# A graph layer on one core: the first loads are asked for earlier, and two more groups of edges are brought by ScalarE and VectorE

## The chip, the cores and the metric

The kernel runs on one core of a Trainium2 chip. The core has five engines with queues of their own: TensorE (PE, with weight loads as PEld), VectorE (DVE), ScalarE (ACT), GpSimd (POOL) and SyncE (SP), which here only issues DMAs. The metric is the device time of one execution in microseconds, the median of several.

## The reference

One layer of a graph network over 12,500 nodes and 400,000 edges, with edges sorted by their target:

```python
h = jnp.maximum(_layernorm(x, axis=-1), 0.0)          # 12500 x 128
s, d = edge_index                                      # 400000 each, d sorted
m = relu(concat([h[s], h[d], edge_attr_32], -1) @ w1 + b1) @ w2 + b2
agg = segment_sum(m, d, num_segments=12500)
gi = agg @ w_ih + b_ih ; gh = h @ w_hh + b_hh          # gates r, z, n of a GRU
out = x + (1 - z) * n + z * h
```

The product with w1 is split: the part of the source is A = h @ w1[0:128], that of the target with the bias is B = h @ w1[128:256] + b1, and the part of the edge's 32 features stays a product per edge. w2 is applied after the sum, per node.

## The kernel before

**First stage.** Nodes come in 14 batches (`load`, L370). VectorE makes the statistics, ScalarE the normalised rows, TensorE turns them and multiplies them with w1; A is written back to memory (`A<-asb`, L482), and three batches of B (`batch_store`). The turned h of all nodes stays on the chip as `hT_all`. The loop runs over 26 chunks, `q`, of up to four tiles. In it also the edge sources of some groups are loaded, one row of 1024 numbers each (`at_row`, L423).

**Edges.** The 3125 tiles of 128 edges make NP = 391 groups of eight (group 0 has five), and each group two units `u`. For each group three things are loaded by SP: for every two groups a tile `L` (`fetch`, L567), which has the places of the targets in its upper 64 partitions (`dstP`, each row copied to 32 partitions) and the features of the edges in the lower 64; and for every group 2 x 32 rows of B into one of four tiles `RW` (`window_rows`, L600), whose lower half holds the weights of the features. VectorE makes a one-hot of the places in `L` (L586), and one product of `L` and `RW` gives the target's and the features' part for 256 columns (L683, tile `pre`). The source's part comes in one of these ways:

- from GpSimd: eight indirect gathers of 128 rows of A into a tile `G` (L163, 11 buffers); VectorE adds it to the product, with the relu (L713). The first nine groups are gathered from x instead, because A is not there yet, and are normalised and turned;
- by ScalarE ("act", 28 groups): 1024 copies of one column of `hT_all` each into `HE_act` (L979), 16 numbers of columns per register load. TensorE multiplies the tile with w1 into `pre` (L694) and ScalarE does the relu (L725);
- by VectorE ("dve", 27 groups): 512 instructions that join two columns each (L986) and 8 copies that part them again (L991) into `HE_dve`;
- by SP ("sp", 5 groups): 1024 DMAs of one row of A each (L968).

After the relu in `RB`, TensorE sums the edges of a node with another one-hot (`seg`, L739). Every 14 groups a block of nodes is finished (`node`, L790): gates, sigmoid, tanh, output, and one batch of B for later groups.

**Order.** The schedule is written by hand: each engine does its instructions in the order of the program, unit after unit (`stages`, L1040; the loop at L1075). `run_jobs` (L1007) spreads a job by hand evenly over the units of its span, four portions per unit. A job for group k ends at unit 2k − 4, four units before the group's first unit; the next one of the same engine starts there. `SPREAD`, `START` and the loop at L92 choose the groups:

```python
SPREAD = {"dve": 27, "act": 28, "sp": 5}
START = {"dve": 14, "act": 4, "sp": 24}
...
        lo, hi = START[m] // 2 + 2, NP - {"dve": 5, "act": 3, "sp": 12}[m]
        for i in range(n):
            k = lo + int((i + 1) * (hi - lo) / n)
```

With this ScalarE has groups 17, 31, 45, ... 388, VectorE 22, 36, ... 386, and the spans have 26 or 28 units. The pool `pj` holds `HE_act` and `HE_dve`, two buffers each, and lies beside the first stage's tiles; the pool `p3`, which holds the three buffers of `L`, takes the memory that the first stage gives back. The first loads for the edges stand after the first stage (L1032):

```python
    gathers(0)
    dst_tile(1)
    for q in range(3):
        fetch(q)
    for k in range(4):
        window_rows(k)
```

Of the kernel before, what the change touches and what calls it, by code (L numbers as in the profile page):

```python
# [11 lines left out]
I32 = mybir.dt.int32  # L12
# [40 lines left out]
PIECE = 128  # L53
STEP = {"act": 4, "dve": 8, "sp": 4}
ROW = 4 * D
SPREAD = {"dve": 27, "act": 28, "sp": 5}
START = {"dve": 14, "act": 4, "sp": 24}
NR = 12672

H_AT = 16512  # L60

# [2 lines left out]
def tile_gnn(ctx: ExitStack, tc: tile.TileContext, x, src, srcT, dstT, dstP, eaT, eaP, w1, b1, w2T, b2,  # L64
# [23 lines left out]
        return [(t0 + a * GRP + j, j, a) for j in (2 * h, 2 * h + 1) for a in range(2)  # L88
                if t0 + a * GRP + j < t1]

    mode, order = {}, {m: [] for m in SPREAD}
    for m, n in SPREAD.items():  # L92
        lo, hi = START[m] // 2 + 2, NP - {"dve": 5, "act": 3, "sp": 12}[m]
        for i in range(n):
            k = lo + int((i + 1) * (hi - lo) / n)
            while k in mode:
                k += 1
            mode[k] = m
            order[m].append(k)


    src_i = {}
# [86 lines left out]
    nc.vector.memset(brow, 0.0)  # L189
    b1b = const.tile([128, D], F32, name="b1b")  # L190
    base_d = at[96:97, :NP - 1]
    by_hand = [k for m in ("sp", "act", "dve") for k in order[m]]
    NJ = len(by_hand)
    place_of = const.tile([NJ, 2], F32, name="place_of")
    for i, (to_sp, to_others) in enumerate(((ROW, 4), (0, H_AT))):
# [107 lines left out]
    def setup(pool):  # L303
# [45 lines left out]
        yield  # L349
        place(0)  # L350

    st_all = const.tile([128, NT, 2], F32, name="st_all")
    nc.vector.memset(st_all[:, NFULL, :], 0.0)
    with tc.tile_pool(name="pp", bufs=3) as pp:
# [85 lines left out]
        for q in range(NC + 3):  # L440
            if q < NC:
                b, i0, c, e, P, n0 = chunk(q)
                if c == 0:
                    stat(b + 2)
                    fin(b + 1)
            if 1 <= q <= NC:
                b, i0, c, e, P, n0 = chunk(q - 1)
                pts[q - 1] = SEGB[q % 2]
                for j in range(c, e):
                    nc.tensor.transpose(pts[q - 1][:, (j - c) * P:(j - c + 1) * P],  # L450
                                        xs[b][:P, j, :], ident[:P, :P])
                if e == bats[b][1]:
                    load(b + 5)
            if q >= 3:
                b, i0, c, e, P, n0 = chunk(q - 3)
                if c == 0:
                    asb[b] = pp.tile([128, 8, D], F32, name="asb", bufs=2)
                nc.scalar.copy(asb[b][:P, c:e, :], pas.pop(q - 3)[:P, :e - c, :])
            if q < NC:
                b, i0, c, e, P, n0 = chunk(q)  # L460
                for j in range(c, e):
                    relu_norm(xs[b][:P, j, :], xs[b][:P, j, :], st_all[:P, i0 + j, :])
                if e == bats[b][1]:
                    sqr(b + 2)
            if 1 <= q <= NC:
                b, i0, c, e, P, n0 = chunk(q - 1)
                copy = nc.scalar.copy if q % 4 == 0 else nc.vector.tensor_copy
                copy(columns(b, c, e), pts.pop(q - 1)[:, :(e - c) * P].rearrange(
                    "f (i p) -> f i p", i=e - c))
            if q >= 4:  # L470
                for _ in range(3):
                    at_row()
            if q >= 6:
                next(setting, None)
            if q in (6, 8, 10):
                batch_product(q // 2 - 3, pp, "bt", 1)
            if q in (7, 9, 11):
                batch_store(q // 2 - 3)
            if q >= 3:
                b, i0, c, e, P, n0 = chunk(q - 3)  # L480
                if e == bats[b][1]:
                    nc.sync.dma_start(nodes(A, i0, e, P), asb[b][:P, :e, :])  # L482
            if 2 <= q <= NC + 1:
                b, i0, c, e, P, n0 = chunk(q - 2)
                pas[q - 2] = ps2.tile([128, PAIR, D], F32, name="pre")
                for j in range(c, e):
                    nc.tensor.matmul(pas[q - 2][:P, j - c, :], columns(b, j, j + 1)[:, 0, :],
                                     w1a, start=True, stop=True)
# [72 lines left out]
        nc.vector.tensor_copy(flag, f[:, 6:7])  # L561


    Ls, OH, RT, HE, SEG = ({} for _ in range(5))
    hand = {}

    def fetch(q):  # L567
        if q * QP >= NP:
            return
        n = min(QP, NP - q * QP)  # L570
        c = slice(q * QP * 512, (q * QP + n) * 512)
        Ls[q] = p3.tile([128, QP * 512], F32, name="L")
        p = dstP[:, c]
        nc.sync.dma_start(
            Ls[q].bitcast(I32)[:2 * V, :n * 512],
            bass.AP(tensor=p.tensor, offset=p.offset, ap=[list(p.ap[0]), [0, V], [1, n * 512]]))
        nc.sync.dma_start(Ls[q][2 * V:, :n * 512], eaP[:, c])

    def onehot_T(k):
        if k >= NP:  # L580
# [8 lines left out]
                                    accum_out=dlast[:2 * V, n:n + 1])  # L589


    bases = {}

    def block(k):
        return max(b for b in range(NB) if BLOCKS[b][0] <= k)

    def slot(b, i):
        return i // 2 if b < NB - 1 else (BP - BLOCKS[b][1]) // 2 + i // 2

    def window_rows(k):  # L600
        if k >= NP:
            return
        b = block(k)
        k0, n, _ = BLOCKS[b]
        if k == k0:
            _, vals = nc.values_load_multi_w_load_instructions(
                base_i[0:1, b, 0:n], engines=[ET.SP], min_val=0, max_val=4 * D * LAST,
                skip_runtime_bounds_check_because="clamped above")
            for i, v in enumerate(vals):
                bases[k + i] = v  # L610
        v = bases.pop(k)
        for a in range(2):
            nc.sync.dma_start(RW[k % 4].bitcast(U8)[V * a:V * (a + 1), a, :],
                              B_bytes[bass.ds(v + 4 * D * SHIFT * a, 4 * D * V)].rearrange(
                                  "(p f) -> p f", p=V))

    def onehot(k):
        if k >= NP or (k % 2 and k > 1):
# [330 lines left out]
    def one_by_one(m, k):  # L949
        et = {"act": ET.Activation, "dve": ET.DVE, "sp": ET.SP}[m]  # L950
        r = by_hand.index(k)
        if m == "sp":
            goal[k] = tc.alloc_semaphore(f"brought{r}"), 16 * PAIR * 128
            G[k] = pj.tile([128, GRP, 2, D], F32, name="G_sp", bufs=1)
            rows = G[k].bitcast(U8)
        else:
            hand[k] = pj.tile([128, PAIR * 128], F32, name=f"HE_{m}")
            he = hand[k].bitcast(U8)
        for e0 in range(0, PAIR * 128, LOAD[m]):
            low, high = (0, ROW * (N - 1)) if m == "sp" else (H_AT, H_AT + 4 * (N - 1))  # L960
            _, vals = nc.values_load_multi_w_load_instructions(
                at[r:r + 1, e0:e0 + LOAD[m]], engines=[et], min_val=low, max_val=high,
                skip_runtime_bounds_check_because="src holds numbers of nodes")
            if m == "sp":
                for i, v in enumerate(vals):
                    e = e0 + i
                    a, j = divmod(e // 128, GRP)
                    fetched = nc.sync.dma_start(rows[e % 128:e % 128 + 1, j, a, :],  # L968
                                                A_bytes[bass.ds(v, ROW)].rearrange("(o f) -> o f", o=1))
                    fetched.then_inc(goal[k][0], 16)  # L970
                    tc.no_tile_sem_insts.add(fetched.ins.name)
                    tc.add_to_no_dep_group(f"rows{k}", fetched.ins)
                    if i % STEP[m] == STEP[m] - 1:
                        yield
                continue
            if m == "act":
                for i, v in enumerate(vals):
                    e = e0 + i
                    nc.scalar.copy(he[:, e * 4:e * 4 + 4], column(v))  # L979
                    if i % STEP[m] == STEP[m] - 1:  # L980
                        yield
                continue
            if e0 % PIECE == 0:
                both = pj.tile([128, PIECE // 2, 4], U16, name="both")
            for i in range(0, LOAD[m], 2):
                nc.vector.scalar_tensor_tensor(both[:, (e0 % PIECE + i) // 2, :], column(vals[i + 1]),  # L986
                                               256.0, column(vals[i]), op0=ALU.mult, op1=ALU.add)
                if i % STEP[m] == STEP[m] - 2:
                    if (e0 + i + 2) % PIECE == 0:
                        p0 = e0 + LOAD[m] - PIECE  # L990
                        nc.vector.tensor_copy(  # L991
                            he[:, p0 * 4:(p0 + PIECE) * 4].rearrange("p (n c b) -> p n c b", c=2, b=4),
                            both.bitcast(U8).rearrange("p n (b c) -> p n c b", c=2))
                    yield
# [12 lines left out]
    def run_jobs(u, phase):  # L1007
        if phase == 0:
            for m, k, span in jobs.get(u, ()):
                live[m] = [one_by_one(m, k), u, span, PAIR * 128 // STEP[m], 0]  # L1010
        for m, job in list(live.items()):
            it, start, span, steps, done = job
            want = -(-steps * ((u - start) * PH + phase + 1) // (span * PH))
# [17 lines left out]

    gathers(0)  # L1032
    dst_tile(1)
    for q in range(3):
        fetch(q)
    for k in range(4):
        window_rows(k)


    def stages(u):  # L1040
# [248 lines left out]
```

## Time and profile before

| | us |
|---|---|
| median of 3 runs | 3385.01 (3376.61 to 3388.27) |
| the profiled execution | 3383.87 |
| its span | 3382.1 |

| engine | busy us | share of the span |
|---|---|---|
| PE | 2400.4 | 71% |
| DVE | 2213.6 | 65% |
| ACT | 3081.1 | 91% |
| POOL | 2542.8 | 75% |

In the rows of the profile the columns are: line, engine, operation, tile written and tiles read, count, then busy time in us and the mean of one in ns, then the idle time of the engine just before these instructions and what ended it. "issue" is idle time in which the engine waited for nothing that the profile shows, such as register loads of its own sequencer; these are not counted as busy. In a timeline a row has its start and its length in us, and in brackets the idle time before it. In a row of a table of stretches stand the stretch, its length, the busy time and count of PE, PEld, DVE, ACT and POOL, the clock granted to TensorE as a part of full speed, the busy share of the 16 DMA engines and GB/s. A row of waits has who waited, on what, the total in us, how often, and the longest.

### The profile page before, as it was taken

The numbers are of one execution on the slowest core, as the hardware profiler recorded it, in microseconds if no ns is written. First come the engines' busy times: TensorE is split into PE (matmuls) and PEld (weight loads), VectorE is DVE, ScalarE is ACT, GpSimd is POOL, SyncE is SP. The second block draws the span as 40 slices with busy tenths as digits, with TensorE's granted clock in tenths as the row PEclk, the third lists the DMA queues.
The fourth block names the chain that finished last, engine by engine and source line by source line (L and its number), as shares of the span: only waits on it lengthen the run. The fifth ranks groups of instructions, "written<-read, shape, count | busy, mean of one in ns | idle before, by whom it ended". The sixth has DMA issues, their size and how long they took to land. (4 is left out here: it accounts for less than half of the span.)

```text
span 3382.1 us, 93395 instructions
## 1 busy us (share of the span) xinstructions
PE 2400.4 (71%) x13113; PEld 1554.8 (46%) x13113; DVE 2213.6 (65%) x16274; ACT 3081.1 (91%) x29057; POOL 2542.8 (75%) x2654
## 2 busy tenths in 40 slices
PE   7567766776677677668776777677667767766767
PEld 6444444444444444445444444444444444444445
DVE  8566666766666666666667766666656666666665
ACT  7599899999999998998999999999889998988975
POOL 7777777777777777777777777777777777777775
PEclk9778777887888777877877878787777787778778
DMA  6433444444444444444444444444444444343332
GB/s 215 104 92 84 95 99 101 99 97 103 96 95 99 97 98 95 99 104 97 96 98 97 98 95 105 97 99 98 95 98 96 100 95 99 94 96 94 92 94 67
DMA packets 196737, 335.77 MB, mean 99 GB/s; under 512 B 69445, under 2 KB 118148, under 8 KB 196112
## 3 DMA queue, kind: packets, MB, share of 16 engines
q0 software_dynamic: 84640, 173.51, 23.0%
q1 hardware_dynamic: 111327, 156.18, 17.8%
q14 instruction: 517, 4.23, 0.4%
q8 instruction: 109, 1.79, 0.2%
q10 hardware_dynamic: 144, 0.07, 0.0%
HBM read 309.25 MB, written 20.24 MB: 97 GB/s over the span
## 5 line engine op out<-in xcount | busy, mean ns | idle before, releaser
L163 POOL DMA_INDIRECT G<-A,src_i x2576 | 2475.8, 961 | 790.4 <-issue 761.2
L979 ACT COPY HE_act<-hT_all 128x4 uint8 x28672 | 2889.0, 189 | 52.9 <-issue 29.1
L986 DVE SCALAR_TENSOR_TENSOR both<-hT_all 128x4 uint16 x13824 | 1174.3, 154 | 930.3 <-issue 925.6
L683 PE MATMUL pre<-RW,L 128*128 128x256 f32 x3128 | 1136.1, 489 | 461.3 <-DMA RW<-B 237.7
L683 PEld LDWEIGHTS pre<-RW,L 128*128 128x128 f32 x3128 | 662.8, 237 | 736.8 <-issue 420.2
L739 PE MATMUL seg<-RB,OH 128*32 128x129 f32 x6250 | 592.7, 319 | 244.2 <-DVE RB L713 211.9
L739 PEld LDWEIGHTS seg<-RB,OH 128*32 128x32 f32 x6250 | 328.0, 123 | 590.7 <-DVE RB L713 310.1
L713 DVE CUSTOM_DVE_ANT_0 RB<-pre,G 128x1024 f32<-128x1024 f32 x323 | 391.1, 1211 | 70.9 <-DMA G<-A,src_i 56.5
L586 DVE TENSOR_SCALAR L<-L,node_of 64x512 f32<-64x512 int32 x382 | 185.9, 487 | 62.2 <-DMA L<-in_dstP 59.9
L725 ACT ACTIVATE RB<-pre 128x1024 f32<-128x1024 f32 x64 | 65.0, 1016 | 91.0 <-PE pre L694 91.0
L633 DVE TENSOR_TENSOR OH<-dloc,seg 128x512 f32<-128x512 f16 (+1 forms) x198 | 132.3, 669 | 0.0
L765 PE MATMUL nd<-spot,sums 128*128 128x40 f32 x782 | 119.6, 326 | 3.6 <-DVE sums L748 3.6
L765 PEld LDWEIGHTS nd<-spot,sums 128*128 128x128 f32 x782 | 115.5, 237 | 12.7 <-issue 8.8
L991 DVE COPY HE_dve<-both 128x512 uint8<-128x512 uint8 x216 | 97.6, 452 | 7.4
L244 PE MATMUL nd<-w1b,hT_all 128*128 128x128 f32 x224 | 49.4, 368 | 73.1 <-DVE xb L850 73.1
L734 PE MATMUL seg<-zrow 1*128 1x129 bf16 x196 | 45.5, 232 | 78.1 <-DVE OH L633 78.0
L694 PEld LDWEIGHTS pre<-w1a,HE_dve 128*128 128x128 f32 x432 | 89.1, 255 | 12.4
L694 PEld LDWEIGHTS pre<-w1a,HE_act 128*128 128x128 f32 x448 | 85.9, 238 | 11.0
L694 PE MATMUL pre<-w1a,HE_dve 128*128 128x128 f32 x432 | 85.4, 333 | 0.0
L694 PE MATMUL pre<-w1a,HE_act 128*128 128x128 f32 x448 | 83.7, 319 | 0.0
L163 POOL DMA_INDIRECT G<-in_x,src_i x69 | 65.6, 950 | 21.9 <-issue 20.7
L244 PEld LDWEIGHTS nd<-w1b,hT_all 128*128 128x128 f32 x224 | 35.2, 231 | 85.5 <-DVE xb L850 80.0
(177 smaller groups left out, 1346.2 us busy)
## 6 DMA issues: line engine op xcount, KB each, us to landing
G_sp<-A SPq DMA_DIRECT2D x5120, 0.5 KB
L<-in_dstP SPq DMA_DIRECT2D x195, 256.0 KB
L<-in_eaP SPq DMA_DIRECT2D x195, 256.0 KB
G<-A,src_i POOLq DMA_INDIRECT x2576, 2.5
RW<-B SPq DMA_DIRECT2D x782, 16.0 KB
xb<-in_x SPq DMA_DIRECT2D x26, 256.0 KB
out<-xb SPq DMA_DIRECT2D x26, 256.0 KB
xs<-in_x SPq DMA_DIRECT2D x11, 512.0 KB
```

Of the source, the lines that this page charges most:

```text
L163: fetched = nc.gpsimd.indirect_dma_start(out=G[k][:, j, a, :], out_offset=None, in_=table, in_offset=bass.IndirectOffsetOnAxis(ap=src_i[c] ...
L244: nc.tensor.matmul(pm[:m, i:i + D], hT_all[:, n0 + i:n0 + i + m], w1b, start=True, stop=True)
L586: nc.vector.tensor_scalar(o, i, node_of[:, k:k + 1], None, op0=ALU.is_equal)
L633: nc.vector.tensor_tensor(p, dloc[:, e0:e1, None].to_broadcast(shape), row[:, None, :].to_broadcast(shape), op=ALU.is_equal)
L683: nc.tensor.matmul(p[:, 2 * i:2 * i + 2, :], Ls[k // QP][:, c0:c0 + 128], RW[k % 4], start=True, stop=not raw)
L694: nc.tensor.matmul(p[:, 2 * i + a, :], cols, w1a, start=False, stop=n + 1 == len(l) or l[n + 1][1] != j)
L713: made = nc.vector._custom_dve(TENSOR_ADD_SAT, out=o, in0=p, in1=G[k].rearrange("p j a f -> p (j a) f")[:, c, :], s0=float("inf"), s1=0.0)
L739: nc.tensor.matmul(p[r0:r0 + V, :D + 1], OH[k][:, a * GRP + j, :], RB[k % 2][:, 2 * j + a, :D + 1], start=False, stop=all(b != a for _, _, ...
L765: nc.tensor.matmul(p[:, bass.ds(offs[i], V + SHIFT)], sums[:, slot(b, i), :D], spot[:, i % 2, :], start=False, stop=i == len(offs) - 1)
L979: nc.scalar.copy(he[:, e * 4:e * 4 + 4], column(v))
L986: nc.vector.scalar_tensor_tensor(both[:, (e0 % PIECE + i) // 2, :], column(vals[i + 1]), 256.0, column(vals[i]), op0=ALU.mult, op1=ALU.add)
L991: nc.vector.tensor_copy(he[:, p0 * 4:(p0 + PIECE) * 4].rearrange("p (n c b) -> p n c b", c=2, b=4), both.bitcast(U8).rearrange("p n (b c) ...
```

## The change

It has two parts.

The first loads for the edges move into the first stage. `fetch` and `window_rows` are defined before it, at q = 16 the rows of B of groups 0 to 3 are asked for, and at q = 18, 20 and 22 the tiles `L` of groups 0 to 5. Since the pool of `L` is not open then, the first two of these tiles are the two buffers of `HE_dve` and the third is one of `HE_act`. The block at L1034 to L1037 goes.

ScalarE has 29 groups instead of 28, VectorE 27 as before, and group 389 (NP − 2) is brought by both: ScalarE copies columns 0 to 511 and VectorE brings 512 to 1023 into one tile of the name `HE_dve`. The groups are spread anew, over 29.5 and 27.5 shares up to group 389: ScalarE's spans are 26 units but for one of 24 and three of 28, and 12 for its half; VectorE's are 26 and 28, and 14 for its half. GpSimd gathers 329 groups instead of 331.

```diff
-SPREAD = {"dve": 27, "act": 28, "sp": 5}
+SPREAD = {"dve": 27, "act": 29, "sp": 5}
+SHARED, CUT = NP - 2, 512
...
-    mode, order = {}, {m: [] for m in SPREAD}
+    def share(m, k):
+        return (0, PAIR * 128) if k != SHARED else (0, CUT) if m == "act" else (CUT, PAIR * 128)
+
+    mode, order = {SHARED: "both"}, {m: [] for m in SPREAD}
     for m, n in SPREAD.items():
-        lo, hi = START[m] // 2 + 2, NP - {"dve": 5, "act": 3, "sp": 12}[m]
+        lo, hi = START[m] // 2 + 2, NP - 12
+        part = 0
+        if m != "sp":
+            hi, part = SHARED, (share(m, SHARED)[1] - share(m, SHARED)[0]) / (PAIR * 128)
         for i in range(n):
-            k = lo + int((i + 1) * (hi - lo) / n)
+            k = lo + int((i + 1) * (hi - lo) / (n + part))
...
+        order[m] += [SHARED] if part else []
...
+        if q < 3:
+            Ls[q] = pj.tile([128, QP * 512], F32, name="HE_dve" if q < 2 else "HE_act")
+        else:
+            Ls[q] = p3.tile([128, QP * 512], F32, name="L")
...
+            if q == 16:
+                for k in range(4):
+                    window_rows(k)
+            if q in (18, 20, 22):
+                fetch((18, 20, 22).index(q))
...
-            hand[k] = pj.tile([128, PAIR * 128], F32, name=f"HE_{m}")
+            if k not in hand:
+                hand[k] = pj.tile([128, PAIR * 128], F32, name="HE_dve" if k == SHARED else f"HE_{m}")
             he = hand[k].bitcast(U8)
-        for e0 in range(0, PAIR * 128, LOAD[m]):
+        for e0 in range(*share(m, k), LOAD[m]):
...
     gathers(0)
     dst_tile(1)
-    for q in range(3):
-        fetch(q)
-    for k in range(4):
-        window_rows(k)
```

More of the change, by code (lines that the diff above doesn't have):

```diff
@@ L191, in tile_gnn @@
     base_d = at[96:97, :NP - 1]
-    by_hand = [k for m in ("sp", "act", "dve") for k in order[m]]
+    by_hand = order["sp"] + order["act"] + [k for k in order["dve"] if k != SHARED]
     NJ = len(by_hand)
@@ L350, in setup, with fetch, block, window_rows @@
         place(0)
+    Ls = {}
+    def fetch(q):
+        if q * QP >= NP:
+            return
+        n = min(QP, NP - q * QP)
+        c = slice(q * QP * 512, (q * QP + n) * 512)
+        if q < 3:
+            Ls[q] = pj.tile([128, QP * 512], F32, name="HE_dve" if q < 2 else "HE_act")
+        else:
+            Ls[q] = p3.tile([128, QP * 512], F32, name="L")
+        p = dstP[:, c]
+        nc.sync.dma_start(
+            Ls[q].bitcast(I32)[:2 * V, :n * 512],
+            bass.AP(tensor=p.tensor, offset=p.offset, ap=[list(p.ap[0]), [0, V], [1, n * 512]]))
+        nc.sync.dma_start(Ls[q][2 * V:, :n * 512], eaP[:, c])
+    bases = {}
+    def block(k):
+        return max(b for b in range(NB) if BLOCKS[b][0] <= k)
+    def window_rows(k):
+        if k >= NP:
+            return
+        b = block(k)
+        k0, n, _ = BLOCKS[b]
+        if k == k0:
+            _, vals = nc.values_load_multi_w_load_instructions(
+                base_i[0:1, b, 0:n], engines=[ET.SP], min_val=0, max_val=4 * D * LAST,
+                skip_runtime_bounds_check_because="clamped above")
+            for i, v in enumerate(vals):
+                bases[k + i] = v
+        v = bases.pop(k)
+        for a in range(2):
+            nc.sync.dma_start(RW[k % 4].bitcast(U8)[V * a:V * (a + 1), a, :],
+                              B_bytes[bass.ds(v + 4 * D * SHIFT * a, 4 * D * V)].rearrange(
+                                  "(p f) -> p f", p=V))
     st_all = const.tile([128, NT, 2], F32, name="st_all")
@@ L561, in check_windows @@
         nc.vector.tensor_copy(flag, f[:, 6:7])
-    Ls, OH, RT, HE, SEG = ({} for _ in range(5))
+    OH, RT, HE, SEG = ({} for _ in range(4))
     hand = {}
[L567 to L577, printed above, removed]
     def onehot_T(k):
@@ L589, in onehot_T @@
                                     accum_out=dlast[:2 * V, n:n + 1])
-    bases = {}
-    def block(k):
-        return max(b for b in range(NB) if BLOCKS[b][0] <= k)
     def slot(b, i):
         return i // 2 if b < NB - 1 else (BP - BLOCKS[b][1]) // 2 + i // 2
[L600 to L615, printed above, removed]
     def onehot(k):
@@ L1009, in run_jobs @@
             for m, k, span in jobs.get(u, ()):
-                live[m] = [one_by_one(m, k), u, span, PAIR * 128 // STEP[m], 0]
+                e0, e1 = share(m, k)
+                live[m] = [one_by_one(m, k), u, span, (e1 - e0) // STEP[m], 0]
         for m, job in list(live.items()):
```

## The prediction

> **What bounds the kernel now.** I read the page for the sums, then the start's timeline, the busy time by stretch, and the waits of ScalarE and VectorE early and late.
>
> ```profile
> span 3382.1 us, 93395 instructions
> L163 POOL DMA_INDIRECT G<-A,src_i x2576 | 2475.8, 961 | 790.4 <-issue 761.2
> L979 ACT COPY HE_act<-hT_all 128x4 uint8 x28672 | 2889.0, 189 | 52.9 <-issue 29.1
> L986 DVE SCALAR_TENSOR_TENSOR both<-hT_all 128x4 uint16 x13824 | 1174.3, 154 | 930.3 <-issue 925.6
> L713 DVE CUSTOM_DVE_ANT_0 RB<-pre,G 128x1024 f32<-128x1024 f32 x323 | 391.1, 1211 | 70.9 <-DMA G<-A,src_i 56.5
> L725 ACT ACTIVATE RB<-pre 128x1024 f32<-128x1024 f32 x64 | 65.0, 1016 | 91.0 <-PE pre L694 91.0
> L991 DVE COPY HE_dve<-both 128x512 uint8<-128x512 uint8 x216 | 97.6, 452 | 7.4
> ```
>
> GpSimd's gathers: 2475.8 busy plus 790.4 before them is 3266.2 us for 2576, 1.268 each, and nearly all of the 790.4 is "issue", its own rhythm. Its first and last gather of A, from the view of that line:
>
> ```profile
> L163 POOL DMA_INDIRECT G<-A,src_i x2576: 940/944/1601, 92.8 to 3355.0; - x199
> ```
>
> So GpSimd works without a break from 92.8 to 3356, and the rest of the kernel ends 26 us later. But it is not the bound everywhere. Waits of VectorE and ScalarE, first for 142.6 to 2272 us, then for 2272 to 3347.6:
>
> ```profile
> DVE L L586 <- DMA L<-in_dstP: 50.2, 21, 5.9
> ACT gt L824 <- PE nd L818: 44.9, 10, 9.0
> ACT RB L725 <- PE pre L694: 26.2, 15, 5.0
> ACT gt L836 <- PE misc L818: 2.0, 1, 2.0
> ACT gt L834 <- DVE gt L831: 0.2, 1, 0.2
> ```
> ```profile
> DVE RB L713 <- DMA G<-A,src_i: 56.3, 26, 4.4
> ACT RB L725 <- PE pre L694: 60.7, 10, 12.4
> ACT gt L824 <- PE nd L818: 18.3, 9, 3.7
> ACT gt L834 <- DVE both L986: 4.2, 1, 4.2
> ```
>
> VectorE waits for gathered rows only after 2272 us. Until then GpSimd is ahead and the other engines set the pace among themselves; they catch up, and from 2272 on GpSimd sets it. The first add of a gathered group is late because the pipeline starts late:
>
> ```profile
> L713 DVE CUSTOM_DVE_ANT_0 RB<-pre,G x323: 680/1215/1226, 203.6 to 3361.7; 128x1024 f32<-128x1024 f32 x161, 128x512 f32<-128x512 f32 x1
> ```
>
> The start, in order of time:
>
> ```profile
> 90.21 0.66 SPq L574 DMA_DIRECT2D L<-in_dstP  x1
> 92.84 0.94 POOL L163 DMA_INDIRECT G<-A,src_i  x1 [3.18 <-DMA L<-in_dstP]
> 100.32 0.48 DVE L586 TENSOR_SCALAR L<-L,node_of 64x512 f32<-64x512 int32 x1 [9.76 <-DMA L<-in_dstP]
> 118.39 1.19 PE L683 MATMUL pre<-RW,L 128*128 128x256 f32 x2 [11.73 <-DMA RW<-B]
> 124.86 0.94 POOL L163 DMA_INDIRECT G<-A,src_i  x1 [2.34 <-PE misc L666]
> ```
>
> After the first stage VectorE stands 9.76 us for the first L, then TensorE 11.73 us for B's rows, and this even costs GpSimd 2.34 us for a buffer. By stretch (busy time of each engine, clock, DMA share, GB/s):
>
> ```profile
> 0.00:88.70 88.70, 67.56 (x320) 62.19 (x320) 71.92 (x376) 61.77 (x144) 66.03 (x77) 0.96 0.67 212
> 142.60:3347.60 3205.00, 2284.26 (x12480) 1457.43 (x12479) 2102.74 (x15709) 2995.44 (x28857) 2433.19 (x2532) 0.79 0.41 97
> 3347.60:3382.10 34.50, 24.36 (x171) 15.84 (x169) 9.29 (x20) 2.73 (x6) 6.49 (x7) 0.91 0.10 27
> ```
>
> 142.6 and 3347.6 are the first and last column copy of ScalarE. Its waits between them are the two lists above: 73.3 + 83.2 = 156.5 us. So ScalarE works 3205.0 − 156.5 = 3048.5 us there.
>
> **The change, part by part.**
>
> *Early loads.* L of groups 0 to 5 and the four RW tiles are issued in the first stage, into buffers that nobody holds then. The two stalls, 9.76 + 11.73 = 21.5 us, go; what is next late is VectorE's own statistics work, which the 21.5 leave in place. SP's queue gets 6 L issues, 8 RW issues and one register load ahead of the last stores of A, and two more rows of edge sources of 4 KB. At 0.66 us for an L issue (row above) and less than that for the rest, below 14 × 0.66 = 9 us spread over some 25 us, in which SP also waits for ScalarE's copies; GpSimd's first gather of A stands behind those stores (its 3.18 us wait). The bytes: 1.7 MB, which at the 212 GB/s of the first row is 8.0 us of the DMA engines. Their share there is 0.67, so a third of the time is free and most of this fits. Bounds: 0 and 8.0 later; I take 2, nearer to 0 because of that free third. Without the cover the full 8 falls on everything.
>
> [...] With no free share, the start would give 21.5 − 8 and not 21.5 − 2. The trace shows 0.67, not 1, and so stands with the smaller cost.
>
> *GpSimd.* 60 groups by other means become 62 (29 + 27 + 5 + the shared one), 16 gathers fewer: 16 × 1.268 = 20.3 us. With the 2.34 us, its work ends 22.6 us earlier: 3382.1 − 22.6 = 3359.5 plus the 2 above, if nothing else is slower. What is next late is ScalarE.
>
> *ScalarE.* 1.5 more groups. One costs 2889.0/28 = 103.2 us of copies and 52.9/28 = 1.9 us before them: 105.1. So 157.6, plus two more relus (57 groups by hand after 55) at 1.016: 159.6. Its work becomes 3048.5 + 159.6 = 3208 us, as long as the stretch with all its waits was. It starts 21.5 earlier, at 121.1, and without any wait ends its last copy at 3329. Then the tail: the last job now is for group 389, not 388. From TensorE's first products for 389 to the end it was
>
> ```profile
> 3352.72 1.03 PE L683 MATMUL pre<-RW,L 128*128 128x256 f32 x4
> ```
>
> 3382.1 − 3352.7 = 29.4 us, with TensorE at work most of it (24.36 of the last 34.5); eight products with copied columns are added, under 1 us. That gives 3329 + 30 = 3359 without waits.
>
> How many waits stay? ScalarE's jobs ran from unit 4 to 772, 384 groups: 7.94 us of work per group. Until 2272 it waited 73.3 of 2129 us, so the others took 3.4% longer than its work, 8.2 us per group. Afterwards 3208/385 groups is 8.33 us: ScalarE turns from 3.4% faster to 1.5% slower than the others. A wait of its at a relu or a gate needs TensorE to be late; now TensorE will mostly stand in front of ScalarE's columns. But the spans are not even: most of its jobs have 26 units, three have 28, and the check of the windows at group 371 sits in one of them; before, the longest single wait was 12.4 us. Bounds for the waits: 0, and 73.3 at the old rate over 3208 us, 110. I take 8, two thirds of one such longest wait, nearer to 0 because the order of speeds turned.
>
> *VectorE.* Half a group: 256 combinations at (1174.3 + 930.3)/13824 = 0.152 us and 4 copies of 0.452 us, 40.8 us; two adds of 1.21 fewer. Spread over 380 groups this is 0.1 us per group on 8.2. It stays under ScalarE's 8.33, barely: its waits (50.2 us for L in the first stretch) are its cover. On the path: nothing by itself; if the cover were gone, 40.8 − 2.4 = 38 us.
>
> *SP's gathers, the shared tile.* Five groups as before, one at 162 instead of 160: nothing. Group 389's tile is written by two engines in separate halves; if either were ordered behind the other the cost would lie at the end, at most one job's length of 14 units.
>
> **Sum.** ScalarE's path sets the end: 3359 + 2 (first stage) + 8 (waits) = 3369 of span; GpSimd's own 3359.5 + 2 stays below it. The profiled execution took 3383.87 for a span of 3382.1 (1.8 around it) and the median is 3385.01 (1.1 more), so I predict 3369 + 1.8, about **3371 us**, and compare it with 3385. A difference under 0.3%, 10 us, can hardly be told from none here: the three runs lie 11.7 us apart.
>
> **Rivals.**
>
> 1. *GpSimd stays the bound.* ScalarE's waits vanish and the first stage takes the loads without cost. Then 3359.5 + 1.8 = 3361. For it: GpSimd's rhythm is steady (median 944 ns, minimum 940). Against: ScalarE has no reserve at all in this case, and three engines would have to stay within a few us of each other.
> 2. *The gates' waits stay: slower.* ScalarE waits at L824 for TensorE's product of the gate, 44.9 us in 2129. If that comes from where the product stands in TensorE's order, behind loads that SP is late with (L586's 50.2 us), and not from ScalarE being ahead, it stays at its rate: 44.9 × 3208/2129 = 68 us. Then 3359 + 2 + 68 + 1.8 = 3431. It decides against the forecast from 37 us of waits on. Against: after 2272, where ScalarE is held at the relus, the gates fall to 18.3.
> 3. *The loads only move the wait.* They take their full 8 us between the stores of A, and GpSimd and the pipeline start 8 later: 3359 + 8 + 8 + 1.8 = 3377, no difference that can be told. For it: the last stores of A are issued at the end of the first stage, so any delay goes to the path. Against: the share of 0.67.
>
> **How the numbers follow.** Forecast 0.47 (3362 to 3384; of it 0.33 faster, 0.14 same). Rival 1: 0.18, faster. Rival 2: 0.20, slower. Rival 3: 0.15, same. Sum: faster 0.51, same 0.29, slower 0.20. Range 3357 to 3400: from just below rival 1 to some 40 us of waits; the rest of rival 2 lies above. The forecast's own range stands beside it because cases of both signs hold most of the chance.
>
> **What would show it.** The start: the first products of line 683's form near 97 us, ScalarE's first column copy near 121, VectorE's first add near 182, GpSimd's buffer wait gone and its first gather of A still near 93 to 95. The middle: ScalarE's waits per job near zero, TensorE waiting in front of the copied columns, VectorE hardly waiting for gathered rows even late. The end: GpSimd's last gather near 3335 and ScalarE's last copy near 3340. Wrong would be: ScalarE's waits over 40 us, a first stage that ends after 92, GpSimd waiting for buffers, or ScalarE's copies taking more than 105 us per group.

## The result and the profile after

The changed kernel takes 3404.23 us (median of nine executions, 3394.55 to 3413.15) where the kernel before takes 3382.74 us in as many. The ratio is 1.0057 with a 95% interval of 1.0047 to 1.0067: slower by 0.6%, where 3371 us and a gain were predicted. The profiled execution of it took 3395.27 us for a span of 3393.5 us, 11.4 us more than the span before.

Groups of instructions from the page of the changed kernel (line, engine, operation, tiles, count, busy us and mean ns, idle time before them and what ended it):

```profile
span 3393.5 us, 95329 instructions
L171 POOL DMA_INDIRECT G<-A,src_i x2560 | 2461.8, 962 | 800.8 <-issue 757.1
L998 ACT COPY HE_act<-hT_all 128x4 uint8 x29696 | 2995.6, 189 | 52.0 <-issue 27.8
L731 DVE CUSTOM_DVE_ANT_0 RB<-pre,G 128x1024 f32<-128x1024 f32 x321 | 388.1, 1209 | 9.7 <-PE pre L701 7.5
L743 ACT ACTIVATE RB<-pre 128x1024 f32<-128x1024 f32 x66 | 66.8, 1012 | 9.3 <-PE pre L712 9.3
```

VectorE's adds no longer wait for gathered rows (56.5 us before, not in the list now), and ScalarE's relus wait 9.3 us instead of 91.0. So GpSimd no longer sets the pace, and ScalarE, which now hardly waits, does, as forecast; how small its lead over the others is, the run with a quarter below shows. What did not come is the early start. First and last start of GpSimd's gathers of A, of ScalarE's column copies and of VectorE's adds, from the views of these lines and of the tile `RB`:

```profile
L171 POOL DMA_INDIRECT G<-A,src_i x2560: 940/947/1674, 110.4 to 3351.8; - x197
L998 ACT COPY HE_act<-hT_all x29696: 177/189/200, 139.6 to 3302.9; 128x4 uint8 x200
L998 ACT COPY HE_dve<-hT_all x512: 178/189/194, 3303.1 to 3358.9; 128x4 uint8 x171
L731 DVE CUSTOM_DVE_ANT_0 RB<-pre,G x321: 679/1214/1226, 199.8 to 3372.6; 128x1024 f32<-128x1024 f32 x160, 128x512 f32<-128x512 f32 x1
```

GpSimd's first gather of A comes at 110.4 instead of 92.8, 17.6 us later; ScalarE's first copy at 139.6 instead of 142.6 and VectorE's first add at 199.8 instead of 203.6, only 3 to 4 us earlier. The end of the first stage shows why. ScalarE's copies of A into `asb` (two buffers) in order of time:

```profile
74.12 0.59 ACT L505 COPY asb<-pre 128x512 f32<-128x512 f32 x1 [1.36 <-DMA A<-asb]
85.13 0.59 ACT L505 COPY asb<-pre 128x512 f32<-128x512 f32 x1 [5.76 <-DMA A<-asb]
96.46 0.59 ACT L505 COPY asb<-pre 128x512 f32<-128x512 f32 x1 [6.99 <-DMA A<-asb]
106.26 0.75 ACT L505 COPY asb<-pre 128x512 f32<-128x512 f32 x2 [7.06 <-DMA A<-asb]
```

It waits there for the store that has to free the buffer, 21.9 us in all, against 0.7 before. The stores are late twice. First, they are issued late: the copies that complete a buffer end at 71.23, 77.82, 87.92 and 98.83, and their stores are issued at 74.96, 85.37, 97.81 and 103.96, 4 to 10 us later, where the kernel before issues them within 0.1 us. At the first, SP issues the load and the rows of edge sources ahead of it; at the others it also stands behind the landing of the loads of places, twice in front of rows of edge sources and once in front of the last stores (from SP's waits between 50 and 130 us):

```profile
SPq L470 <- DMA HE_dve<-in_dstP: 14.4, 2, 8.1
SPq L534 <- DMA HE_act<-in_dstP: 5.1, 1, 5.1
```

Second, they land late. The DMAs of that stretch, worked out from the semaphore events of the trace (issue time in us, transfer, distinct events of its landing, us from issue to landing); ahead of each store stands the load of places issued just before it:

```
changed kernel                             kernel before
72.54 HE_dve<-in_dstP   3 events   9.8      71.34 A<-asb  16 events  3.1
74.96 A<-asb           16 events  10.1      76.86 A<-asb  16 events  3.2
82.94 HE_dve<-in_dstP   3 events  11.5      81.62 A<-asb  16 events  2.8
85.37 A<-asb           16 events  11.0      86.31 A<-asb  16 events  2.7
95.31 HE_act<-in_dstP   3 events   8.6      90.21 L<-in_dstP   3 events  10.1
97.81 A<-asb           16 events   8.4      91.65 L<-in_dstP   3 events  16.6
103.96 A<-asb          16 events   3.7      93.02 L<-in_dstP   3 events  23.7
```

A load of places is 256 KB and lands with two or three events, where the store of 512 KB lands with sixteen. Its source pattern has the two rows of `in_dstP` as the outermost step, then 32 copies of each. In the first stage of the changed kernel it takes 8.6 to 11.5 us, with the first of its three events after 1.0 to 1.2 and the other two at 8.1 or later; three at once, as in the kernel before, take 10.1, 16.6 and 23.7 us. What is issued behind it lands in two parts: of the sixteen events of the stores issued at 74.96, 85.37 and 97.81, fourteen come 2.5 to 4.6 us after the issue and the last two only after 7.4 to 11.0. So it is in the kernel before with the first four loads of B's rows behind the three loads of places: all events but two within 2.2 us, the last two after 16 to 18. My reading is that the load runs on two DMA engines of sixteen, and that the stores have a share on those two and land with it. The traces do not name the engine of an event, so this is inferred from the counts; that the shape of the load decides is shown by the runs with it split, below.

The whole span in three stretches (start, ScalarE's copies, rest), busy us and count of PE, PEld, DVE, ACT and POOL, clock, DMA share, GB/s, and ScalarE's waits in the middle one:

```profile
0.00:139.60 139.60, 95.76 (x467) 83.07 (x468) 101.28 (x547) 82.56 (x196) 89.62 (x102) 0.84 0.57 169
139.60:3358.90 3219.30, 2314.30 (x12535) 1464.13 (x12534) 2120.70 (x15967) 3150.00 (x30394) 2439.61 (x2537) 0.79 0.41 97
3358.90:3393.50 34.60, 25.74 (x147) 16.61 (x147) 9.11 (x20) 2.80 (x8) 0.00 (x0) 0.80 0.04 10
```
```profile
ACT gt L842 <- PE nd L836: 12.8, 6, 6.6
ACT RB L743 <- PE pre L712: 1.9, 2, 1.0
ACT gt L854 <- PE misc L836: 0.8, 2, 0.5
ACT HE_act L998 <- ACT HE_act L998: 0.7, 3, 0.4
```

The waits are 16.2 us, so ScalarE works 3219.3 − 16.2 = 3203.1 us.

### The profile page after: what moved, and what is told of

Read it like the earlier page. It is cut to its first block, busy times and chain, and to the rows that moved or that the text cites. A ratio compares the mean times of both kernels' runs of the same rounds, so it can differ in the third digit from the quotient of the medians.

```text
span 3393.5 us, 95329 instructions
## 1 busy us (share of the span) xinstructions
PE 2435.8 (72%) x13145; PEld 1563.8 (46%) x13145; DVE 2231.1 (66%) x16532; ACT 3235.4 (95%) x30595; POOL 2529.2 (75%) x2638
## 5 line engine op out<-in xcount | busy, mean ns | idle before, releaser
L998 ACT COPY HE_act<-hT_all 128x4 uint8 x29696 | 2995.6, 189 | 52.0 <-issue 27.8
L1005 DVE SCALAR_TENSOR_TENSOR both<-hT_all 128x4 uint16 x14080 | 1192.4, 154 | 966.6 <-issue 956.7
L757 PE MATMUL seg<-RB,OH 128*32 128x129 f32 x6250 | 608.3, 326 | 298.6 <-DVE RB L731 207.6
L626 DVE TENSOR_SCALAR L<-L,node_of 64x512 f32<-64x512 int32 x376 | 184.8, 491 | 34.3 <-DMA L<-in_dstP 33.7
L752 PE MATMUL seg<-zrow 1*128 1x129 bf16 x196 | 45.8, 234 | 138.0 <-DVE OH L651 137.9
L832 PE MATMUL nd<-DEG,brow 34*128 34x512 f32 (+2 forms) x112 | 70.9, 716 | 45.5 <-ACT gt L842 45.5
L712 PEld LDWEIGHTS pre<-w1a,HE_dve 128*128 128x128 f32 x448 | 81.2, 226 | 9.6
```

What stands on the lines that cost most here:

```text
L626: nc.vector.tensor_scalar(o, i, node_of[:, k:k + 1], None, op0=ALU.is_equal)
L712: nc.tensor.matmul(p[:, 2 * i + a, :], cols, w1a, start=False, stop=n + 1 == len(l) or l[n + 1][1] != j)
L757: nc.tensor.matmul(p[r0:r0 + V, :D + 1], OH[k][:, a * GRP + j, :], RB[k % 2][:, 2 * j + a, :D + 1], start=False, stop=all(b != a for _, _, ...
L832: nc.tensor.matmul(pg, brow[:, c], DEG[:, :w], start=True, stop=False)
```

## The experiments

Theories at the start. *Mine:* ScalarE is the bound of the changed kernel from its first copy on, and the early loads delay the stores of A, which eats the gain at the start. *Rival on the loads:* not the loads but the rows of edge sources delay the stores: the changed kernel has more of them ahead of its last stores on SP's queue. *Rival on the spread:* GpSimd's sixteen gathers fewer decide, and the new spread alone is a gain.

In the runs e1 to e4 and e9 to e16 the kernel before, measured beside them, takes 5695 to 5743 us instead of 3383; they are told last. The others are comparable to the result above.

### The rows of edge sources

Six rows at a time in place of three, so that fewer of them are left for the end of the stage:

```diff
-                for _ in range(3):
+                for _ in range(6):
                     at_row()
```

> The changed kernel with the rows of edge sources asked for six at a time, a second time, on a chip where the kernel before takes 3383 and not 5695 us. Theory (SP's queue, by way of the rows behind L's landing): first gather of A at 92 to 96 us, ScalarE's first copy at 121 to 124, the end at 3377 to 3382. Rival (the 1.7 MB hold up the stores of A): first gather at 105 or later, 3395 or more.

Measured: 3399.76 us, ratio to before 1.0056, 1.0040 to 1.0073: no better than the changed kernel, and what the rival expected. ScalarE's first copy comes at 135.4 and GpSimd's first gather of A at 106.2, 4.2 us earlier each. The three loads of places are now issued closer together (71.5, 73.5 and 78.6) and take 12.4, 19.5 and 21.5 us; the stores behind them take 13.4, 16.8 and 12.7. SP no longer stands behind their landing: the waits of 14.4 and 5.1 us are not in its list now, and each store is issued as soon as its buffer is complete. So the rows, and SP's standing in front of them, were worth 4 us. The rest comes from the stores' landing; whether the bytes as such hold it up, as the rival has it, or the shape of the load, the next runs tell.

### The places' load in two

The same 256 KB as two DMAs of one row each, whose outermost step is the 32 copies:

```diff
-        nc.sync.dma_start(Ls[q].bitcast(I32)[:2 * V, :n * 512],
-            bass.AP(tensor=p.tensor, offset=p.offset, ap=[list(p.ap[0]), [0, V], [1, n * 512]]))
+        for a in range(2):
+            nc.sync.dma_start(Ls[q].bitcast(I32)[V * a:V * (a + 1), :n * 512],
+                bass.AP(tensor=p.tensor, offset=p.offset + a * list(p.ap[0])[0],
+                        ap=[[0, V], [1, n * 512]]))
```

In e6 the changed kernel has this for the three early tiles alone, in e7 for all; in e8 the kernel before has it for all.

> The changed kernel; the load of the places into L (2 rows of memory, each copied to 32 partitions) is made of two DMAs of 32 partitions for the first three tiles. In the traces that load signalled its landing from only 2 or 3 events where the others have 16, took 8 to 12 us, and whatever was issued behind it landed late too. Theory (the load runs on two of the 16 DMA engines and the stores of A have their shares behind it there): split, it lands in 3 to 5 us, the stores of A in 3 to 5 us again instead of 8 to 17, the first gather of A comes at 92 to 96, ScalarE's first copy at 121 to 125, the end at 3375 to 3382. Rival (the bytes as such, or the loads beside the stores on all engines): the stores still land in 8 us or more, first gather at 102 or later, 3392 or more.

> The changed kernel with that load in two DMAs for all 196 tiles. Theory: start as in the run with the first three split; in the edges' stage the waits of VectorE for L (33.7 us in the changed kernel) and of TensorE for RW (165.5) shrink, but ScalarE is the bound there, so 3370 to 3382. Rival (SP's queue, with 196 more issues, becomes late): TensorE's waits for RW grow, 3390 or more.

> The kernel before with that load in two DMAs for all tiles; nothing of the change. Theory: L and RW after the first stage land 10 to 15 us earlier (they landed at 100 to 118), the pipeline starts that much earlier, but GpSimd still sets the end and gains only its 2.3 us: 3376 to 3383. Rival (SP late): 3390 or more.

| | median us | ratio to before | interval |
|---|---|---|---|
| e6, changed, three tiles | 3379.57 | 1.0000 | 0.9981 to 1.0018 |
| e7, changed, all tiles | 3374.42 | 0.9982 | 0.9964 to 1.0001 |
| e8, before, all tiles | 3373.61 | 0.9981 | 0.9960 to 1.0002 |

The gathers and ScalarE's copies of e6, then of e8, from the views of their lines:

```profile
L171 POOL DMA_INDIRECT G<-A,src_i x2560: 939/947/1637, 97.5 to 3335.6; - x197
L1005 ACT COPY HE_act<-hT_all x29696: 176/189/199, 126.7 to 3291.1; 128x4 uint8 x200
```
```profile
L163 POOL DMA_INDIRECT G<-A,src_i x2576: 940/947/1532, 91.9 to 3356.2; - x199
L981 ACT COPY HE_act<-hT_all x28672: 177/189/198, 125.8 to 3343.7; 128x4 uint8 x200
```

In e6 the early halves land in 3.6 to 4.6 us with 15 or 16 events, and the stores of A behind them in 3.8 to 4.6; the first gather of A is at 97.5 and the first copy at 126.7, 13 us before that of the changed kernel. Nothing but the shape of three loads was changed. That shows the cause of 13 of the 16.5 us by which the start came late; the rows of edge sources are some 4 more, which fits e17 below, where both are mended and the first copy comes at 122.5. The first gather and the first copy of e6 are still 1.5 and 1.7 us later than expected, and e8 is 2.4 us faster than expected.

e8 is the other half of it. Without any early load, the split alone brings the first copy of the kernel before from 142.6 to 125.8: the two stalls that the change was to remove fall from 21.5 to 4.5 us (VectorE for the first `L` 2.7, TensorE for B's rows 1.8), so most of them came from the shape of these loads. And e8's median gains no more than 0.2%, which its interval does not tell from none, since GpSimd still gathers until 3356.2 and VectorE waits for gathered rows again (`DVE RB L715 <- DMA G<-A,src_i` is 65.8 us over its run): an earlier start of the pipeline alone moved nothing behind GpSimd here.

### The new spread alone

The early loads go back behind the first stage, the spread stays:

```diff
-            if q == 16:
-                for k in range(4):
-                    window_rows(k)
-            if q in (18, 20, 22):
-                fetch((18, 20, 22).index(q))
...
     dst_tile(1)
+    for q in range(3):
+        fetch(q)
+    for k in range(4):
+        window_rows(k)
```

> The new spread without the early loads. On a chip where the kernel before takes about 3383: my theory (ScalarE is the bound from its first copy on) has the first copy at 142.6 as before and then the changed kernel's work, waits and tail: 142.6 + 3219 + 34.6 + 1.8 = 3398, ratio 1.0045. Rival (GpSimd's 16 fewer gathers decide): 3362 to 3372, ratio 0.994 to 0.997.

Measured: 3408.36 us (four executions, 3391.36 to 3415.81) against 3377.92, ratio 1.0095, 1.0078 to 1.0111. The rival falls: sixteen gathers fewer bring nothing here, although GpSimd's last gather comes at 3332.5 instead of 3355.0. The loss is twice the expected one. ScalarE's copies, the stretch of them, and its waits in it:

```profile
L990 ACT COPY HE_act<-hT_all x29696: 176/189/198, 142.3 to 3298.7; 128x4 uint8 x200
```
```profile
142.30:3356.80 3214.50, 2285.38 (x12536) 1445.84 (x12535) 2120.99 (x15967) 3146.15 (x30395) 2421.68 (x2522) 0.80 0.41 96
```
```profile
ACT gt L834 <- PE nd L828: 11.8, 5, 7.0
ACT gt L846 <- PE misc L828: 2.4, 2, 2.0
ACT gt L844 <- DVE gt L841: 2.2, 2, 1.5
ACT RB L735 <- PE pre L704: 1.5, 2, 0.9
ACT HE_act L990 <- ACT HE_act L990: 0.9, 2, 0.6
```

The first copy is where it was before, at 142.3. The waits fall from 156.5 to 18.8 us, the work grows from 3048.5 to 3214.5 − 18.8 = 3195.7: 147.2 us of work more fill 137.7 us of waits less. The spread spends ScalarE's whole reserve and 9.5 us beyond it. The span of the profiled execution is 3389.6 us, 7.5 longer than before; the theory has some 3396. But the median is 30 us above the kernel before, and the profiled execution itself only 13; the 17 us between are not explained: the three other executions took 15 to 24 us more than the profiled one, and only that one has a trace.

### A quarter instead of half

In the changed kernel with all loads split and six rows at a time, ScalarE brings a quarter of group 389 and VectorE three quarters:

```diff
-SHARED, CUT = NP - 2, 512
+SHARED, CUT = NP - 2, 256
```

> The changed kernel with the places' loads split in two, six rows of edge sources at a time, and ScalarE a quarter of group 389 instead of half. On a chip where the kernel before takes about 3383: my theory (ScalarE is the bound in the changed kernel and its path is start, work, tail) takes a quarter of a group, 26 us, from ScalarE and some 26 us of span from its last job: about 3355 to 3365, ratio 0.993 to 0.995, ScalarE's first column copy near 126 and its last below 3330. Rival (GpSimd, TensorE and VectorE close behind set the end): 3372 to 3380, no better than the split loads alone.

Measured: 3377.36 us (ten executions), ratio 1.0001, 0.9991 to 1.0011. The rival holds. The views of its lines and of `RB`, and ScalarE's waits while it copies:

```profile
L171 POOL DMA_INDIRECT G<-A,src_i x2560: 940/944/1562, 93.3 to 3329.0; - x197
L1000 ACT COPY HE_act<-hT_all x29696: 176/189/198, 122.5 to 3303.2; 128x4 uint8 x200
L1000 ACT COPY HE_dve<-hT_all x256: 180/189/196, 3303.4 to 3330.7; 128x4 uint8 x128
L733 DVE CUSTOM_DVE_ANT_0 RB<-pre,G x321: 681/1212/1225, 183.7 to 3347.5; 128x1024 f32<-128x1024 f32 x160, 128x512 f32<-128x512 f32 x1
```
```profile
ACT RB L745 <- PE pre L714: 17.4, 6, 11.4
ACT gt L844 <- PE nd L838: 15.4, 6, 6.7
```

Here the start is the one predicted for the change, and the theory on ScalarE still falls: of the 21 us that ScalarE works less than in e7 (3174.8 against 3196.1), its waits take 19 back (33.4 with two small ones, against 14.8): it waits for TensorE again. In this kernel's groups, TensorE waits for VectorE's one-hots and adds, 193.9 and 251.1 us where it was 149.7 and 193.3 in e7, and VectorE has three quarters of a group more by hand than before:

```profile
L1007 DVE SCALAR_TENSOR_TENSOR both<-hT_all 128x4 uint16 x14208 | 1202.4, 153 | 984.1 <-issue 981.2
L754 PE MATMUL seg<-zrow 1*128 1x129 bf16 x196 | 45.8, 234 | 193.9 <-DVE OH L653 193.9
```

VectorE's 2239.8 busy us and the 981 us of "issue" in its combinations are 3221 of 3366.7 us; TensorE's wait for the one-hots was 78.0 before and 137.9 in the changed kernel. So VectorE is likely the next bound, close behind ScalarE and GpSimd. That is read from these sums and was not tested.

### The same questions where every kernel takes 1.7 times as long

In the runs e1 to e4 and e9 to e16 every kernel takes 1.7 times as long. ScalarE's column copies last as long as elsewhere, but they follow each other late; the copies of the loads-only kernel (e1), and its granted clock:

```profile
L996 ACT COPY HE_act<-hT_all 128x4 uint8 x28672 | 3152.8, 189 | 2148.7 <-issue 2121.4
```
```profile
core 0: 5697.2 us, clock 0.669
```

2121.4 us of "issue" stand where the kernel before has 29.1 at 3383 us. It is not ScalarE alone: ahead of VectorE's combinations they are 1618.1 us instead of 925.6. In e1 ScalarE's 3341.7 busy us and these 2121.4 are 5463 of 5697 us, and VectorE's 2308.2 and 1618.1 are 3926. So with the old spread ScalarE is already the bound there, by some 1,500 us, and these runs say nothing of the balance at 3383 us. The loads alone (e1, again as e10 and e14) have the old spread:

```diff
-SPREAD = {"dve": 27, "act": 29, "sp": 5}
-SHARED, CUT = NP - 2, 512
+SPREAD = {"dve": 27, "act": 28, "sp": 5}
+SHARED, CUT = -1, 512
...
-    mode, order = {SHARED: "both"}, {m: [] for m in SPREAD}
+    mode, order = {}, {m: [] for m in SPREAD}
...
-        lo, hi = START[m] // 2 + 2, NP - 12
+        lo, hi = START[m] // 2 + 2, NP - {"dve": 5, "act": 3, "sp": 12}[m]
...
-        if m != "sp":
-            hi, part = SHARED, (share(m, SHARED)[1] - share(m, SHARED)[0]) / (PAIR * 128)
```

The spread alone (e2, again as e9, e13 and e16) and the six rows (e3; with the old spread e4) have the edits above. In e11 the changed kernel has all loads split and the quarter, in e12 and e15 the six rows as well.

> The early loads as in the changed kernel, the groups spread as before (28 by ScalarE, 27 by VectorE, none shared). Theory (the first stage grows because SP's queue stands behind the landing of L): the first gather of A starts near 110 us as in the changed kernel, not at 92.8, and GpSimd with its 2576 gathers sets the end: 17.6 us later than before, less the 2.3 us of its old buffer wait, about 3398. Rival (the new spread of the groups is what costs, the early loads do no harm): 3380 or less.

> The loads after the first stage as before, the groups spread as in the changed kernel (29 and a half, 27 and a half). Theory: ScalarE's first copy at 142.6 as before, then its 3203 us of work and some 16 us of waits, and a tail of 34.6: about 3398, ScalarE the bound, GpSimd waiting for nothing and its last gather near 3336. Rival (the whole loss comes from the first stage): the spread alone is a gain, 3365 to 3372.

> The changed kernel, but the rows of edge sources are asked for six at a time, so that none is left behind the loads of L in SP's queue; same bytes at the same places of the loop. Theory (the queue, by way of the rows that stand behind L's landing): the first gather of A comes back to 92 to 96 us, ScalarE's first copy to 121 to 124, the end to 3377 to 3382. Rival (the 1.7 MB themselves hold up the stores of A on the DMA engines): the first gather of A stays at 105 or later and the time at 3395 or more.

> The early loads with the rows six at a time, the groups spread as before. Theory: the start is 20 us earlier for the pipeline, but GpSimd sets the end and gains only its 2.3 us buffer wait: 3378 to 3383, no difference from before. Rival (the pipeline's start decides): 3362.

> The changed kernel with the places' load in two DMAs for all tiles, and of group 389 ScalarE brings a quarter and VectorE three quarters. Theory (ScalarE is the bound by its work, 105 us a group): 26 us less than with the half, ScalarE's stretch ends near 3313, GpSimd becomes the bound with its last gather at 3330: 3357 to 3364 us. Rival (VectorE, with 20 us more, takes over): 3372 or more.

> The same with the rows of edge sources six at a time. Theory: the stores of A no longer stand behind rows that wait for loads, first gather of A at 93 instead of 97, and with GpSimd as the bound the end 4 us earlier: 3353 to 3360. Rival (the rows make the first batches late): no gain, 3361 or more.

| | ratio to before, measured beside it |
|---|---|
| loads alone: e1, e10, e14 | 1.0018, 1.0010, 1.0028 |
| loads alone, six rows: e4 | 1.0008 |
| spread alone: e2, e9, e13, e16 | 1.0278, 1.0276, 1.0280, 1.0278 |
| whole change, six rows: e3 | 1.0300 |
| split loads, quarter: e11; with six rows e12, e15 | 1.0165; 1.0165, 1.0188 |

One and a half groups more on ScalarE cost 2.8%, one and a quarter 1.7 to 1.9%: the more of ScalarE's work is given back, the less is lost. The expectations' times were worked out for a kernel of 3383 us and are not answered by these runs. The loads alone were not measured where the kernel before takes 3383 us, so what they are worth beside the old spread stays open there.

## Why the prediction was wrong

The sum for the span was 121.1 for the start, 2 for the loads, 3208 of ScalarE's work, 8 of waits and 30 of tail: 3369. Measured in the profiled execution: 139.6 + 3203.1 + 16.2 + 34.6 = 3393.5. By term:

- **Early loads: the step that failed.** "A third of the time is free and most of this fits", 2 us, at most 8. The start came 139.6 − 123.1 = 16.5 us later than that, two thirds of the 24.5 us. The working took the bytes and divided by what all sixteen engines moved on average. But each load of places took 8.6 to 11.5 us for its 256 KB, and the stores of A behind it land in 8.4 to 11.0 us instead of 2.7 to 3.2, fourteen events of sixteen early and two late; the mean share of 0.67 showed none of this. If the load runs on two engines, as its two or three events suggest, what counted was the share on those two. SP's own time was mis-sized too: put at below 9 us of issuing, it stood 19.5 us behind the landing of these loads, though that was worth only 4 us (e5). The trace of before had shown it: the stall for the first `L` (9.76 us) was the landing of such a load, and that for B's rows (11.73 us) the landing of rows issued behind three of them, both quoted and only counted as a gain. The two stalls did go; ScalarE's 21.9 us for `asb` and GpSimd's 20.2 us for the last store took their place. The loss itself is not the loads' alone: the new spread without them (e18) loses 0.95%, the whole change 0.6%. What the loads failed to bring is the 19.5 us that were to outweigh the spread's extra work. Whether, beside this spread, they cost or gain is open: the profiled spans of the two, 3393.5 and 3389.6 us, and the ratios point opposite ways.
- **Rival 3** named the right place, the loads between the stores of A, and its bound of 8 us was too small by a factor of two, for the same reason.
- **ScalarE's work** was right: 3208 predicted, 3203.1 measured, 105 us a group. Its change from the engine with reserve to the one that hardly waits was right too: 16.2 us of waits after 156.5, where 8 was taken, 8.2 too few. That it is the bound by a margin is not shown: in e17, with 21 us less to do, it waits 19 more.
- **Rival 2**, the gates' waits that stay, is refuted: 12.8 us at the gates, not 68.
- **The tail** was mis-sized by 4.6 us. From the first products of the last job by hand, at 3359.85, to the end it took 33.7 us, and 29.4 before, with a clock of 0.80 where it was 0.91.
- **GpSimd** has its sixteen gathers fewer, but starts 17.6 us later, so it ends at 3351.8 and not near 3335. In e17, with a start at 93.3, it ends at 3329.0: that step holds where the loads do not hurt.
- **VectorE's half group** stayed hidden in the changed kernel, as far as ScalarE's waits tell. That its cover is thin ("barely") fits e17, where it has a quarter more and ScalarE waits again; that the one causes the other was not tested.
- **From the span to the time.** The profiled execution lies 9 us below the median of the nine, a term that the sum did not have, and 24 + 9 is the whole miss of 33 us. The same is seen with e5 (3391.38 against 3399.76), e17 (3368.59 against 3377.36) and e18 (3391.36 against 3408.36); but e6, with the same spread, lies 4 us above its median, and the kernel before 1 us above. What sets these executions apart stays open.

With the loads mended (e6, e7) the changed kernel comes to 3380 and 3374 us, within the error of the kernel before. So the predicted 3371 is missed by 9 and 3 us once the step that failed is taken out. That e7's profiled span, 3369.9, is nearly the 3369 of the sum is partly luck: its start is 3 us later than the sum's, its waits 7 and its tail 3 longer, and its work 12 less. And even that is no gain that these runs can tell from none: the forecast ratio was 3371/3385 = 0.996, e7's is 0.998, the split alone gives the kernel before the same (e8), and the new spread alone loses 0.95%.

## What to carry to other kernels

Before a load is moved under other transfers, look at how it lands: few landing events (two or three, where the stores of A had sixteen), and a time that its bytes at the mean rate do not explain (8.6 to 11.5 us for 256 KB, 1.2 by estimate at the 212 GB/s moved in the first 88.7 us of the kernel before), were here the signs of a load that held up the stores issued behind it. Here the pattern of that load was what to mend first: made of two loads of one row each, with the 32 copies outermost, it alone brought the first copy from 142.6 to 125.8 us (e8), most of the stall that the move was made for. And give an engine more work only up to its waits: 157 us of waits were no room for 160 us of work. The spread alone turned 138 us of them into work and gained nothing, and taking 21 us of work back gained nothing either; most likely because GpSimd and VectorE are each within a few per cent of being the bound, which was not tested engine by engine.

## What the runs showed of the hardware

- A 256 KB load that repeats two rows 32 times each lands in 8.6 to 11.5 us with three landing events in the first stage of the changed kernel (the next one, at 120.87, has two and takes 9.5), and three in a row in 10.1, 16.6 and 23.7 us in the kernel before; as two loads of 32 partitions each it lands in 3.6 to 4.6 us with fifteen or sixteen in e6. A 512 KB store issued behind the unsplit load takes 8.4 to 11.0 us instead of 2.7 to 3.2; fourteen of its sixteen events come within 4.6 us.
- The same program took 5695 to 5743 us in some sets of runs instead of 3383, at a granted clock of 0.67 (e1) instead of 0.80. ScalarE's small copies last 189 ns in both; in e1 2121 us of "issue" stand ahead of them instead of 29, and 1618 instead of 926 ahead of VectorE's combinations. What makes it so is not shown, nor that it goes with the chip: e15 and e16 (5743 us) and e17 and e18 (3378 us) are all listed under chip 3.
